# Pair sums behind the transposes, and rotated rows read back from DRAM

## The chip, the cores and the metric

The kernel runs on one core of a Trainium2 chip. The metric is device microseconds of one execution of the whole program (lower is better). The core has five engines that run side by side: TensorE (PE in the profile, with PEld for its weight loads), VectorE (DVE), ScalarE (ACT), GpSimd (POOL) and SyncE (SP, which here only issues transfers). All values are float32.

## The reference, cut to what matters

Eight images of 256 channels and 96 x 96 pixels go through two attention layers, each behind a group norm and with a residual.

```python
# layer 0
x = x + _L0_conv_ref(_gn(x), w1, b1, w2, b2, w3, b3, w_out, temperature)
# layer 1
x = x + _L1_conv_ref(_gn(x), Wq, bq, Wk, bk, Wv, bv)

def _L0_conv_ref(x, ...):
    q_f, k_f, v_f = (fft2(pconv(x, w, b)) for w, b in ((w1, b1), (w2, b2), (w3, b3)))
    # 8 heads of 32 channels; q_f, k_f normalized over the 9216 frequencies
    attn = einsum('bhcn,bhdn->bhcd', q_f, k_f) * temperature
    attn = complex(softmax(real(attn)), softmax(imag(attn)))
    out = abs(ifft2(einsum('bhcd,bhdn->bhcn', attn, v_f)))
    return pconv(out, w_out)

def _L1_conv_ref(x, ...):
    q, k = softplus(Wq x + bq), softplus(Wk x + bk)          # 32 channels
    v = Wv x + bv
    attn_map = einsum('bdn,ben->bde', k, v)
    norm = 1 / einsum('bnd,bd->bn', q, k.sum(-1) + EPS)
    return einsum('bnd,bde,bn->ben', q, attn_map, norm)
```

The product of q_f and k_f has no conjugate, so in pixels it pairs each pixel with its mirror image (row h with row 96 - h, column w with column 96 - w). The kernel therefore needs two Gram matrices of 256 x 256 per image: of e = x + mirrored x, and of o = x - mirrored x, over half of the pixels.

## The kernel before, in words

Channels lie on the 128 partitions, in two halves (KC = 2). Two SBUF arenas hold whole images and swap roles from image to image: one is x, the other holds y of layer 0, later layer 1's k and q, and then takes the next image's x while it is emptied. The rows of an image lie in the arena so that a tile of eight rows t (of NT = 12) holds four rows and their four mirrored rows; `x_col` gives their place. t = 11 is loaded first and t = 0 last.

Each image goes through five stages, and the next image's pair sums are woven into the later ones:

1. **Pair sums** (`pair_sums`): `even_odd` forms e and o for four row pairs at once, with two additions or subtractions of 128 x 760 numbers on POOL or DVE (L317), and small ones for column 0 (L318). Then, 128 pixels at a time, four TensorE transposes (eoT, L350) put the pixels on partitions, ScalarE copies them from PSUM to an xT slot (L353), and eight matmul instructions add their products to the two Gram matrices (acc, L331) one step later. There are 37 such steps per image. Each step also takes its share of the group norm's statistics (L264, DVE).
2. **Attention** (`attention`): a chain of small matmuls and small DVE and ACT operations makes the attention matrix from the Gram matrices, up to `at` (L488) and `mz` (L511).
3. **Rotation** (`rotate`), woven into attention: 48 row pairs. For each, four transposes (xr, L550) put the pixels of the two rows on 96 partitions, ScalarE copies them to an xT slot (L563), and two steps later four y products (L553, two instructions each) multiply them with a window of the table `rt` in DRAM (`tm`, loaded three pairs at a time). DVE copies the result into the y arena (L559) and one column into ys (L558).
4. **Images** (`images`): z (L621) from y, squares and roots, and the projection po (L633) added to x (L635).
5. **Layer 1 and output** (`layer1`, `output`): kq, softplus, kx; then per step four o matmuls (L863), three DVE additions (L868) and one POOL addition (L872) into x, and stores.

The order on the engines comes from generators: `weave(stage, other)` runs as many steps of `other` as the stage yields, so `attention` gives each of its latencies a number of rotation steps, and `images`, `layer1` and `output` do the same with the next image's pair sums; `finish` runs what is left. A planner may reorder instructions outside the blocks of `manual_schedule`; inside them the named engines keep the order of the program: PE in attention, PE, DVE, POOL and SP in the output stage.

```python
        with tc.manual_schedule(engines={mybir.EngineType.PE}):
            weave(attention(b), turns)
            finish(turns)
        sums = pair_sums(b + 1) if b + 1 < B else iter(())
        weave(images(b), sums)
        weave(layer1(b), sums)
```

PSUM has five buffers `ps` for all passing results and three `acc`. SBUF buffers that matter here: the ring of four (e and o tiles, image tiles, weights), three `tm`, and six xT slots, of which the last two serve the pair sums. y's column 0 is copied from x by POOL (L530). x loads, stores, and weights are issued on SP's queue; `tm` for images 1 to 7 on ACT's.

Of the kernel before, what the change touches and what calls it, by code (L numbers as in the profile page):

```python
# [53 lines left out]
P = 128  # L55
KC = 2
# [3 lines left out]
TR = 6  # L60
NZ = 33
# [7 lines left out]
def two_layer_kernel(ctx: ExitStack, tc: tile.TileContext, x, w1t, b1, w2t, b2, w3, b3, wot, temp,  # L69
# [96 lines left out]
    turn = [0, 0]  # L166

    def xt_slot(sums=False):

        turn[sums] += 1  # L170
        return xT[:, NX - 2 + turn[1] % 2 if sums else turn[0] % (NX - 2)]
# [8 lines left out]
    half = const.tile([P, 1], F32, name="half")  # L180
    nc.vector.memset(half, 1.0)
    nc.vector.memset(half[0:W], 0.5 ** 0.5)
# [46 lines left out]
    rt = dram.tile([H, 2 * W], F32, name="rt")  # L229

    def tables():
# [18 lines left out]
        for i in range(2):  # L250
            o = (3 + i) * W
            nc.vector.tensor_copy(t0[:, o:o + 1], r0[:, 0:1])
            nc.vector.tensor_copy(t0[:, o + 1:o + W], r0[:, W - 1:0:-1])
        nc.sync.dma_start(out=rt, in_=t0[:, 3 * W:5 * W])
        load_small()

    def window(h):

        v = rt[h:h + TR, 1:1 + W]
        return bass.AP(v.tensor, v.offset, [[1, W], [2 * W, TR], [1, W]])  # L260

# [34 lines left out]
    def even_odd(b, u):  # L296

        assert (b, u % NT) in loaded
        nr = PR if u < NT else 1
        t = ring_tile(f"eo_{b}_{u}").rearrange("p (c k n) -> p c k n", c=2, k=KC)  # L300
        x_t = image(x_of(b))
        rows = [PR * u + i for i in range(nr)]
        if u in (0, NT):
            parts = [(0, 1)] + ([(1, nr)] if nr > 1 else [])
        else:
            parts = [(0, nr)]
        for lo, hi in parts:
            n = hi - lo
            ra = x_col(rows[lo]) // W
            rp = x_col((H - rows[lo]) % H) // W  # L310
            back = slice(rp, rp - n if rp >= n else None, -1)
            for c in range(2):
                eng = nc.vector if u in (0, 1, NT) or (u == NT // 2 - 1 if b else u % 2) else nc.gpsimd
                op = (eng.tensor_add, eng.tensor_sub)[c]
                pop = (nc.gpsimd.tensor_add, nc.gpsimd.tensor_sub)[c]
                d = t[:, c, :, 0:nr * W].rearrange("p k (h w) -> p k h w", w=W)
                op(d[:, :, lo:hi, 1:W], x_t[:, :, ra:ra + n, 1:W], x_t[:, :, back, W - 1:0:-1])  # L317
                pop(d[:, :, lo:hi, 0:1], x_t[:, :, ra:ra + n, 0:1], x_t[:, :, back, 0:1])  # L318
        return t, nr * W

    s0 = {}

    def pair_sums(b):
# [12 lines left out]

        pending, first = None, True
        us = [*range(NT - 1, -1, -1), NT]
        ahead = [even_odd(b, us.pop(0))]
        for u in range(NT - 1, -2, -1):  # L340
            u %= NT + 1
            eo, cols = ahead.pop(0)
            for i in range(0, cols, P):
                while i == 0 and us and len(ahead) < (2 if b and u in (NT - 3, NT - 4) else 1):
                    ahead.append(even_odd(b, us.pop(0)))
                np_ = min(P, cols - i)
                pt = ps_tile(f"eoT_{b}_{u}_{i}")
                for c in range(2):
                    for k in range(KC):
                        nc.tensor.transpose(pt[0:np_, c * C + k * P:c * C + (k + 1) * P], eo[:, c, k, i:i + np_], ident)  # L350
                t = xt_slot(True)
                weight = half[0:np_] if u in (0, NT) and i == 0 else 1.0
                nc.scalar.activation(t[0:np_, :, 0:C], pt[0:np_, :].rearrange("p (c n) -> p c n", c=2), AF.Copy,  # L353
                                     scale=weight)
                if pending is not None:
                    products(*pending, first, False)
                    first = False
# [608 lines left out]
```

## Time and profile before

| What | Value |
|---|---|
| median of 3 runs | 2763.6 us (2762.03 to 2764.65) |
| the profiled execution's own time | 2762.53 us |
| its span, first to last instruction | 2760.7 us |
| granted TensorE clock, mean | 0.993 |
| PE, PEld, DVE, ACT, POOL busy | 99%, 71%, 71%, 49%, 30% |
| chain that ended last, by engine | PE 94%, DVE 3%, ACT 2%, DMA 1% |
| chain, by line: xr L550, y L553, eoT L350, acc L331 | 6%, 10%, 5%, 13% |
| xr: instructions, mean length | 1520, 275 ns |
| y: instructions, mean length | 3040, 261 ns |
| e and o on POOL, 128 x 760 (L317) | 136, 1809 ns |
| POOL addition of 128 x 384 (L872) | 96, 1004 ns |
| DMA: queues q1 and q10 | 164.34 MB in 129800 packets, 25.12 MB in 67248 |

The profile is of one execution. The busy share of an engine is the time in which it had at least one instruction running. TensorE instructions overlap in the trace, so that the sum or mean of their lengths is more than the time they cost in a row; the spacing of their starts is the better price. The chain follows the last instruction back to what released it at each step. A DMA share is the mean over 16 transfer engines.

### The profile page before, as it was taken

How to read it: one execution, taken by the hardware profiler on the slowest of the kernel's cores; microseconds unless marked ns; L12 is line 12 of the kernel's file. 1: busy time of each engine (PE TensorE's matmuls, PEld its weight loads, DVE VectorE, ACT ScalarE, POOL GpSimd, SP SyncE). 2: the span in 40 equal slices, each digit the busy share in tenths (PEclk: the TensorE clock that was granted, in tenths of full speed). 3: DMA queues.
4: the chain of work that ended last, by engine and by line, in shares of the span. 5: the costliest groups of instructions: out<-in, count | busy, mean ns of one | idle time of the engine just before them, and what ended most of it. 6: DMA issues, size and time to landing. Idle time of an engine off the chain costs nothing.

```text
span 2760.7 us, 47785 instructions
## 1 busy us (share of the span) xinstructions
PE 2719.5 (99%) x18348; PEld 1972.5 (71%) x18348; DVE 1958.4 (71%) x4104; ACT 1366.5 (49%) x2098; POOL 841.5 (30%) x939
## 2 busy tenths in 40 slices
PE   8999999999999999999999999999999999999988
PEld 8965679657795677956679566885678856788556
DVE  7588666876668767587675875769766687676776
ACT  3455634556345563355634546345453455544553
POOL 5033340342403423035230351313513135131311
PEclk9999999999999999999999999999999999999997
DMA  5120151201512015120151201521015210251003
GB/s 169 40 65 11 47 184 43 67 9 49 179 43 73 6 47 182 43 69 6 54 179 46 63 6 54 182 54 52 7 53 184 58 46 7 62 178 28 0 7 138
DMA packets 197274, 192.50 MB, mean 70 GB/s; under 512 B 88821, under 2 KB 197049, under 8 KB 197049
## 3 DMA queue, kind: packets, MB, share of 16 engines
q1 hardware_dynamic: 129800, 164.34, 18.8%
q10 hardware_dynamic: 67248, 25.12, 3.6%
q8 instruction: 146, 2.39, 0.4%
q14 instruction: 80, 0.65, 0.1%
HBM read 113.85 MB, written 75.57 MB: 69 GB/s over the span
## 4 chain that ended last, share of the span: by engine, by line
PE 94%; DVE 3%; ACT 2%; DMA 1%; issue 1%; POOL 0%; SPq 0%; POOLq 0%; DVEq 0%; ACTq 0%
PE z L621 21%; PE po L633 18%; PE acc L331 13%; PE y L553 10%; PE xr L550 6%; PE eoT L350 5%; PE xT L779 5%; PE kq L718 5%; PE o L863 4%; PE kx L755 3%; DMA arena<-in_x_dram 1%; PE cw L423 1%; PE kT L770 1%; DVE arena L559 1%; PE mz L511 1%
## 5 line engine op out<-in xcount | busy, mean ns | idle before, releaser
L621 PE MATMUL z<-arena,mz 128*128 128x384 f32 (+2 forms) x2400 | 595.0, 476 | 0.0
L633 PE MATMUL po<-e,wo 128*128 128x384 f32 x1536 | 529.7, 486 | 0.2 <-ACT e L668 0.2
L667 POOL TENSOR_TENSOR e<-e 128x768 f32<-128x768 f32 x192 | 348.2, 1815 | 554.1 <-ACT e L666 554.1
L621 PEld LDWEIGHTS z<-arena,mz 128*128 128x128 f32 (+1 forms) x2400 | 325.6, 163 | 241.4 <-issue 42.4
L553 PE MATMUL y<-tm,xT 96*128 96x97 f32 x3040 | 472.6, 261 | 1.7 <-ACT sd_a L288 0.5
L553 PEld LDWEIGHTS y<-tm,xT 96*128 96x128 f32 x3040 | 457.8, 192 | 12.5 <-issue 4.9
L331 PE MATMUL acc<-xT 128*128 128x256 f32 (+2 forms) x2368 | 440.5, 328 | 3.5 <-ACT xT L353 3.5
L633 PEld LDWEIGHTS po<-e,wo 128*128 128x128 f32 x1536 | 289.4, 190 | 197.7 <-DVE arena L635 1.2
L662 DVE TENSOR_TENSOR e<-z,xT 128x768 f32<-128x768 f32 x384 | 365.7, 953 | 85.2 <-PE z L621 85.2
L264 DVE BATCH_NORM_STATS2 st<-arena 128x6 f32<-128x384 f32 x768 | 406.5, 552 | 13.7 <-DMA arena<-in_x_dram 3.2
L550 PE MATMUL xr<-ident,arena 128*96 128x128 f32 x1520 | 409.2, 275 | 0.0
L331 PEld LDWEIGHTS acc<-xT 128*128 128x128 f32 (+1 forms) x2368 | 380.2, 191 | 37.7 <-ACT xT L353 5.2
L563 ACT COPY xT<-xr 96x512 f32<-96x512 f32 (+1 forms) x384 | 220.2, 578 | 293.8 <-PE xr L550 289.4
L666 ACT ACTIVATE e<-e 128x1536 f32<-128x1536 f32 x192 | 284.6, 1482 | 93.5 <-DVE e L662 92.3
L668 ACT ACTIVATE e<-e 128x768 f32<-128x768 f32 x192 | 161.9, 843 | 334.0 <-POOL e L667 332.9
L317 POOL TENSOR_TENSOR eo<-arena 128x760 f32<-128x760 f32 x136 | 246.1, 1809 | 253.7 <-issue 130.1
L635 DVE TENSOR_TENSOR arena<-arena,po 128x384 f32<-128x384 f32 x384 | 211.1, 551 | 92.6 <-PE po L633 69.5
L353 ACT ACTIVATE xT<-eoT 128x512 f32<-128x512 f32 x280 | 166.6, 598 | 183.9 <-PE eoT L350 182.2
L550 PEld LDWEIGHTS xr<-ident,arena 128*96 128x96 f32 x1520 | 227.2, 150 | 10.3 <-issue 6.9
L559 DVE COPY arena<-y 128x384 f32<-128x384 f32 (+1 forms) x384 | 209.7, 547 | 1.2 <-issue 0.5
L558 DVE COPY ys<-y 128x4 f32<-128x4 f32 (+1 forms) x384 | 62.4, 162 | 199.3 <-PE y L553 195.9
L350 PE MATMUL eoT<-ident,eo 128*128 128x128 f32 (+1 forms) x1184 | 188.1, 280 | 10.4 <-POOL eo L318 10.4
(202 smaller groups left out, 2907.0 us busy)
## 6 DMA issues: line engine op xcount, KB each, us to landing
arena<-in_x_dram SPq DMA_DIRECT2D x184, 384.0 KB
out_dram<-arena SPq DMA_DIRECT2D x184, 384.0 KB
tm<-rt ACTq DMA_DIRECT2D x112, 216.0 KB
tm<-rt SPq DMA_DIRECT2D x16, 216.0 KB
arena<-in_x_dram SPq DMA_DIRECT2D x8, 288.0 KB
out_dram<-arena SPq DMA_DIRECT2D x8, 288.0 KB
wl<-in_w1t_dram SPq DMA_DIRECT2D x8, 256.0 KB
wl<-in_w2t_dram SPq DMA_DIRECT2D x8, 256.0 KB
```

The source lines that it names most:

```text
L264: nc.vector.bn_stats(out=st[:, k, c, :], in_=x_of(b)[:, k, c * CH:(c + 1) * CH])
L317: op(d[:, :, lo:hi, 1:W], x_t[:, :, ra:ra + n, 1:W], x_t[:, :, back, W - 1:0:-1])
L331: mm = nc.tensor.matmul(acc[c][:, m * C:m * C + (KC - m) * P], lhsT=t[0:np_, c, m * P:(m + 1) * P], rhs=t[0:np_, c, m * P:C], start=(first ...
L350: nc.tensor.transpose(pt[0:np_, c * C + k * P:c * C + (k + 1) * P], eo[:, c, k, i:i + np_], ident)
L550: nc.tensor.transpose(pt[0:W, r * C + k * P:r * C + (k + 1) * P], x_of(b)[:, k, o:o + W], ident)
L553: nc.tensor.matmul(pu[:, o:o + W + 1], lhsT=gt[0:W, r, k * P:(k + 1) * P], rhs=tm[:, g % TR + r, :], start=True, stop=True)
L559: nc.vector.tensor_copy(y[:, :, :, g + r:g + 2], src[:, :, W - 1::-1, r:2])
L621: mm = nc.tensor.matmul(out[:, o:o + n * W], lhsT=columns(mz, k, c, j), rhs=y[:, k, h * W:(h + n) * W], start=(k == 0 and o == 0), stop=(k ...
L633: nc.tensor.matmul(po[:, 0:CH], lhsT=wo[:, k, m * P:(m + 1) * P], rhs=e[:, k, :], start=(k == 0), stop=(k == KC - 1))
L662: nc.vector.tensor_add(e[:, 2 * c:2 * c + 2, :].rearrange("p t (q h) -> p t q h", h=H), pz[:, 0:CH].rearrange("p (q h) -> p q h", h=H).uns ...
L666: nc.scalar.activation(e, e, AF.Square)
L667: nc.gpsimd.tensor_add(e[:, 0:2, :], e[:, 0:2, :], e[:, 2:4, :])
```

## The change

Pair sums: instead of forming e and o and transposing both, each step now transposes 128 pixels of x as they lie in the arena and 128 mirrored pixels, which POOL has copied in reverse order into a small tile `back` (`turn_back`, one step ahead). ScalarE copies both from PSUM into a ring tile, scaled by a column of weights `pw`; e and o are then formed behind it, as sum and difference of the two halves (128 x 256 each), on DVE or on POOL: on POOL for odd j in image 0, and for t < 3 (but for the last step) in the other images. Column 0 of the rows is gathered in a tile `w0` and goes through two mixed chunks at the end, (0, 2) and (0, 3), which POOL puts together from short copies.

For tiles t = 3 to 11 the two halves in the ring tile are stored to a DRAM tile `xtd` (two transfers per step on SP's queue; column 0 by two more behind two transposes of w0). The rotation reads 35 of its 48 row pairs from there into the xT slots (`fetch`, three steps ahead, one transfer of 96 x 2 x 256 numbers, on SP's queue) and does not transpose them; the mirrored rows come in reverse order and are multiplied with a second table `rb`. The row pairs that are still transposed (84 to 94 and 0 to 10, and 48) come first, but for 48. All six xT slots serve the rotation. The two extra tiles of layer 1 (`kxt`) are now taken at the start of the image stage.

```diff
+T0 = 3
...
-    turn = [0, 0]
-    def xt_slot(sums=False):
-        turn[sums] += 1
-        return xT[:, NX - 2 + turn[1] % 2 if sums else turn[0] % (NX - 2)]
+    turn = [0]
+    def sum_slot():
+        turn[0] += 1
+        return xT[:, NX - 2 + turn[0] % 2]
...
+    pw = const.tile([P, 4], F32, name="pw")
+    nc.vector.memset(pw[:, 3:4], 0.0)
...
+    rb = dram.tile([H, 2 * W], F32, name="rb")
+    xtd = dram.tile([2, (H // 2 - PR * T0) * W, C], F32, name="xtd")
...
+            nc.sync.dma_start(out=rb[:, i * W:(i + 1) * W], in_=r0)
...
-    def window(h):
-        v = rt[h:h + TR, 1:1 + W]
-        return bass.AP(v.tensor, v.offset, [[1, W], [2 * W, TR], [1, W]])
+    def window(h, n, back):
+        v = (rb if back else rt)[h:h + n, 0 if back else 1:]
+        return bass.AP(v.tensor, v.offset, [[1, W], [2 * W, n], [1, W]])
+    def turned(c, h, w):
+        return xtd[c, (h - PR * T0) * W + w:]
...
-    def even_odd(b, u):
...
-                op(d[:, :, lo:hi, 1:W], x_t[:, :, ra:ra + n, 1:W], x_t[:, :, back, W - 1:0:-1])
-                pop(d[:, :, lo:hi, 0:1], x_t[:, :, ra:ra + n, 0:1], x_t[:, :, back, 0:1])
...
+        x = x_of(b)
+        w0 = one.tile([P, KC, H + 1], F32, tag="ys", name=f"w0_{b}")
+        nc.gpsimd.memset(w0[:, :, H // 2:H // 2 + 1 + PR * T0], 0.0)
+        def sides(t, j):
+            o = (NT - 1 - t) * TW + (t == 0) * W + 1 + P * j
+            e = (NT - t) * TW - (t == 0) * W - 1 - P * j
+            if t or j < 2:
+                return [(0, P, x[:, :, o:o + P], x[:, :, e:e - P:-1])]
+            m = H // 2
+            rows = [x[:, :, x_col(h):x_col(h) + W] for h in (0, H // 2)] + [w0]
+            if j == 2:
+                return [(0, 32, x[:, :, o:o + 32], x[:, :, e:e - 32:-1])] + [
+                    (32 * i + 32, 32, v[:, :, 1:33], v[:, :, W - 1:W - 33:-1] if i < 2 else w0[:, :, m + 2:m + 34])
+                    for i, v in enumerate(rows)]
+            return [(32 * i, 32, v[:, :, m:m + 32], v[:, :, m:m - 32:-1]) for i, v in enumerate(rows[0:2])] + [
+                (64, 32, w0[:, :, 32:64], None), (64, 16, None, w0[:, :, m + 33:m + 49]), (80, 16, None, w0[:, :, m:m + 16]),
+                (96, 32, rows[0][:, :, 0:32], rows[0][:, :, 0:32])]
+        back = three.tile([P, TR * (W + 1)], F32, tag="tm", name=f"back_{b}")[:, 0:2 * C].rearrange(
+            "p (i k n) -> p i k n", i=2, k=KC)
+        def turn_back(i):
+            t, j = steps[i]
+            assert (b, t) in loaded
+            if j == 0:
+                col = x[:, :, (NT - 1 - t) * TW:(NT - t) * TW:W]
+                h, o = PR * t, H // 2 + 1 + PR * t
+                nc.gpsimd.tensor_copy(w0[:, :, h:h + PR], col[:, :, 0:PR])
+                if t:
+                    nc.gpsimd.tensor_copy(w0[:, :, o:o + PR], col[:, :, :PR - 1:-1])
+                else:
+                    nc.gpsimd.tensor_copy(w0[:, :, o:o + 1], col[:, :, 0:1])
+                    nc.gpsimd.tensor_copy(w0[:, :, o + 1:o + PR], col[:, :, 2 * PR - 2:PR - 1:-1])
+                    nc.gpsimd.tensor_copy(w0[:, :, o - 1:o], col[:, :, 2 * PR - 1:])
+            if j in (0, 3):
+                xts.append(ring_tile(f"xt_{b}_{t}_{j}").rearrange("p (j c n) -> p j c n", j=3, c=2))
+            ab = sides(t, j)
+            ready = len(ab) == 1
+            front = ab[0][2] if ready else xts[-1][:, j % 3, 0].rearrange("p (k n) -> p k n", k=KC)
+            for p0, n, *v in ab:
+                for c in range(ready, 2):
+                    if v[c] is not None:
+                        nc.gpsimd.tensor_copy((front, back[:, i % 2])[c][:, :, p0:p0 + n], v[c])
+            return front, xts[-1][:, j % 3]
+        steps = [(t, j) for t in range(NT - 1, -1, -1) for j in range(3)] + [(0, 3)]
         pending, first = None, True
...
+        xts = []
+        ahead = turn_back(0)
+        for i, (t, j) in enumerate(steps):
+            front, both = ahead
+            if i + 1 < len(steps):
+                ahead = turn_back(i + 1)
+            pt = ps_tile(f"eoT_{b}_{t}_{j}").rearrange("p (c n) -> p c n", c=2)
+            for k in range(KC):
+                nc.tensor.transpose(pt[:, 0, k * P:(k + 1) * P], front[:, k], ident)
+                nc.tensor.transpose(pt[:, 1, k * P:(k + 1) * P], back[:, i % 2, k], ident)
+            nc.scalar.activation(both, pt, AF.Copy, scale=pw[:, j:j + 1])
+            if t >= T0:
+                n = P - j // 2
                 for c in range(2):
-                    for k in range(KC):
-                        nc.tensor.transpose(pt[0:np_, c * C + k * P:c * C + (k + 1) * P], eo[:, c, k, i:i + np_], ident)
-                t = xt_slot(True)
-                nc.scalar.activation(t[0:np_, :, 0:C], pt[0:np_, :].rearrange("p (c n) -> p c n", c=2), AF.Copy,
-                if pending is not None:
-                    products(*pending, first, False)
-                    first = False
-                pending = (t, np_)
-                if u < NT and i:
-                    stats_chunk(st0, b, 2 * (NT - 1 - u) + i // P - 1)
-                yield
+                    nc.sync.dma_start(out=turned(c, PR * t, 1 + P * j)[0:n], in_=both[0:n, c])
+            eo = sum_slot()[:, :, 0:C]
+            if j % 2 if not b else t < T0 and (t or j < 3):
+                nc.gpsimd.tensor_add(eo[:, 0], both[:, 0], both[:, 1])
+                nc.gpsimd.tensor_sub(eo[:, 1], both[:, 0], both[:, 1])
+            else:
+                for c, op in enumerate((ALU.add, ALU.subtract)):
+                    nc.vector.scalar_tensor_tensor(eo[:, c], in0=pt[:, 0], scalar=pw[:, j:j + 1], in1=both[:, 1],
+                                                   op0=ALU.mult, op1=op)
+            if pending is not None:
+                products(*pending, first, False)
+                first = False
+            pending = (eo, P)
+            if j in (1, 2):
+                stats_chunk(st0, b, 2 * (NT - 1 - t) + j - 1)
+            if (t, j) == (T0, 2):
+                n = H // 2 - PR * T0
+                pt = ps_tile(f"w0T_{b}")
+                col = xts[-2][:, 0, 0]
+                for k in range(KC):
+                    nc.tensor.transpose(pt[0:H + 1 - PR * T0, k * P:(k + 1) * P], w0[:, k, PR * T0:H + 1], ident)
+                nc.scalar.copy(col[0:H + 1 - PR * T0], pt[0:H + 1 - PR * T0, 0:C])
+                for c in range(2):
+                    o = c * (H // 2 + 1)
+                    nc.sync.dma_start(out=xtd[c].rearrange("(h w) n -> h w n", w=W)[:, 0], in_=col[o:o + n])
+            yield
...
+            back = H // 2 <= h < H - PR * T0
+            n = 2 if h == H // 2 else 0
+            for lo, hi in ((0, n), (n, TR)) if n else ((0, TR),):
+                (nc.scalar if b else nc.sync).dma_start(out=tm[:, lo:hi, 0:W], in_=window(h + lo, hi - lo, back and lo == n))
             nc.gpsimd.tensor_copy(tm[:, :, W:W + 1], csn[0:W, 2, h:h + TR].unsqueeze(2))
             return tm
 
-        def step(h, turned):
+        order = [*range(H - 2 * TR, H, 2), *range(0, H - 2 * TR, 2)]
+        spilled = [PR * T0 <= h < H - PR * T0 and h != H // 2 for h in order]
+        xts = {}
+        def fetch(i):
+            if i < len(order) and spilled[i]:
+                xts[i] = xT[:, i % NX]
+                h = order[i]
+                c = h > H // 2
+                rows = turned(c, H - h - 1 if c else h, 0)[0:2 * W]
+                nc.sync.dma_start(out=xts[i][0:W, :, 0:C], in_=rows.rearrange("(r w) n -> w r n", w=W))
...
+                back = PR * T0 <= g < H - PR * T0 and g > H // 2
...
-                nc.vector.tensor_copy(y[:, :, :, g + r:g + 2], src[:, :, W - 1::-1, r:2])
+                nc.vector.tensor_copy(y[:, :, :, g + r:g + 2], src[:, :, 0:W, r:2] if back else src[:, :, W - 1::-1, r:2])
...
-        tms = [load_r(g) for g in range(0, 3 * TR, TR)]
+        pieces = order[::TR // 2]
+        tms = [load_r(g) for g in pieces[0:3]]
+        pieces = pieces[3:]
         pending = []
-        for h in range(0, H, 2):
-            if h % TR == 0:
+        for i, h in enumerate(order):
+            if i % (TR // 2) == 0:
                 tm = tms.pop(0)
-            if h % TR == 4 and 3 * TR <= h - 4 + 2 * TR < H:
-                tms.append(load_r(h - 4 + 2 * TR))
-            xt = step(h, pending.pop(0) if len(pending) == 2 else None)
-            pending.append((h, xt, tm))
+            if h % TR == 4 and i > TR // 2 and pieces:
+                tms.append(load_r(pieces.pop(0)))
+            if not spilled[i]:
+                xts[i] = xT[:, i % NX]
+            step(None if spilled[i] else h, pending.pop(0) if len(pending) == 2 else None, xts[i])
+            pending.append((h, xts.pop(i), tm))
+            fetch(i + 3)
...
+        kxt[b] = [three.tile([P, TR * (W + 1)], F32, tag="tm", name=f"xt{i}_{b}")[:, 0:2 * (C + 2)].rearrange(
+            "p (j n) -> p j n", j=2) for i in range(2)]
+        for t in kxt[b]:
+            nc.gpsimd.memset(t[:, :, C:C + 2], 1.0)
...
-        extra = [three.tile([P, TR * (W + 1)], F32, tag="tm", name=f"xt{i}_{b}")[:, 0:2 * (C + 2)].rearrange(
-            "p (j n) -> p j n", j=2) for i in range(2)]
-        for t in extra:
-            nc.gpsimd.memset(t[:, :, C:C + 2], 1.0)
...
```

## The prediction

> **What bounds the kernel now.** I read the busy shares first, then the chain of waits, then TensorE's waits, then the timeline where the change acts.
>
> ```profile
> PE 2719.5 (99%) x18348; PEld 1972.5 (71%) x18348; DVE 1958.4 (71%) x4104; ACT 1366.5 (49%) x2098; POOL 841.5 (30%) x939
> PE 94%; DVE 3%; ACT 2%; DMA 1%; issue 1%; POOL 0%; SPq 0%; POOLq 0%; DVEq 0%; ACTq 0%
> PE eoT L350 <- POOL eo L318: 10.4, 15, 7.3
> PE at L488 <- DVE arena L559: 1.1, 7, 0.2
> ```
>
> TensorE is busy 99% and is 94% of the chain that ended last. The two waits (total us, times, longest) say that it hardly ever waits, but the second shows a place where seven images arrive with no slack: the attention matmul `at` is just late for VectorE. So work taken off TensorE is worth its issue time, wherever nothing else becomes late.
>
> How much issue time is a transpose? The busy column misleads: the rows of L550 (409.2 us) and L553 (472.6) count overlapping instructions. I take start-to-start times (start, length, engine, instruction), at the end of one image's rotation:
>
> ```profile
> 486.05 0.27 PE L550 MATMUL xr<-ident,arena 128*96 128x128 f32 x1
> 486.17 0.36 PE L553 MATMUL y<-tm,xT 96*128 96x97 f32 x2
> 486.36 0.27 PE L550 MATMUL xr<-ident,arena 128*96 128x128 f32 x1
> 486.47 0.36 PE L553 MATMUL y<-tm,xT 96*128 96x97 f32 x2
> 486.67 0.27 PE L550 MATMUL xr<-ident,arena 128*96 128x128 f32 x1
> 486.78 2.15 PE L553 MATMUL y<-tm,xT 96*128 96x97 f32 x18
> ```
> ```profile
> 486.67 2.09 PEld L553 LDWEIGHTS y<-tm,xT 96*128 96x128 f32 x18
> ```
>
> One transpose plus one y product (two instructions) takes 0.31 us; a row pair has four of each, 1.24 us. In the last line 18 y instructions run without transposes: (2.15 - 0.26)/17 = 0.111 us each, and the weight loads keep the same pace, (2.09 - 0.19)/17 = 0.112. So y alone is bound by its weight loads, and a pair without transposes costs 8 x 0.111 = 0.89 us. Taking four transposes away saves **0.35 us per pair**, not the 0.45 that four times their 0.11 spacing suggests.
>
> **What the Trainium skill says.** "Perfetto Trace Analysis", Identifying the Most-Contended Engine: matmul busy share is a poor measure, weight-load share a better one; here 99% against 71%, and the overlap above agrees. "TensorE: Matmul & The Clock Gate", LDWEIGHTS: columns/1.2 ns, so 107 ns for 128 columns; the 112 ns above agrees. "GPSIMD Engine Reference", 3.1 Elementwise: 2.6 cycles per element for two inputs, 2.2 ns at its 1.2 GHz; the trace's (1815 - 1004)/384 = 2.1 ns per element (768- and 384-wide adds, L667 and L872) agrees. [...]
>
> **Part 1, rotation: the gain.** In the built program the xr transposes fall from 1520 to 400: 35 pairs x 4 x 8 images = 1120. 35 x 0.35 x 8 = **-98 us**. The 280 ScalarE copies of 0.58 us that go too were hidden behind TensorE.
>
> **Part 2, what the rotation uncovers: +32.** Attention's latencies are hidden behind rotation steps, and 36 of the 48 become shorter. Between `ssq` and `at` VectorE works without a break in the timeline: 10.5 us for reciprocals, softmax pieces and seven or eight y copies (0.54 us per pair back to back), in nearly the same order in the new program. TensorE covers it today with eight 1.24 us steps; at 0.89 it arrives 2.8 us early, of which I keep 2 as a wait. The short hops after it (one step of cover each) give 1 more. The fetches: each brings 192 packets of 1 KB. Queue q1 spent 18.8% of 16 engines' span on 129800 packets, 64 ns for 1266 B; at 1 KB I estimate 52 to 64 ns, so 0.62 to 0.77 us of all 16 engines per pair. The `tm` windows (q10: 23.6 ns x 576 packets per three pairs) add 0.28. Sum 0.90 to 1.05 against 0.89 on TensorE: in the last 16 pairs, where no attention work is left, the transfers are level with TensorE or a little slower[...]. I take 1. Together 4 us per image (bounds 1.5 and 8).
>
> **Part 3, pair sums in mid-image: +14 for seven images.** Transposes (4 per step, 37 steps) and acc products are the same. What moves is before and behind them. POOL gets one reversed 128x256 copy per step: 0.34 us by the slope of its small copies, 0.65 by L530's strided 128x192 copy (0.525 us); I take 0.4. e and o, formerly one set of large operations per three steps, come behind ScalarE's copy: two VectorE operations of 128x256, estimated 0.36 us each from the 0.49 spacing of the 384-wide adds of L868. In the output stage (the 40 us before attention):
>
> ```profile
> 712.00:720.00 8.00, 8.00 (x60) 5.68 (x59) 5.44 (x13) 2.96 (x7) 4.33 (x6) 1.00 0.61 203
> 720.00:728.00 8.00, 8.00 (x61) 5.71 (x60) 6.05 (x14) 2.97 (x7) 6.52 (x6) 1.00 1.03 374
> 728.00:736.00 8.00, 8.00 (x61) 5.71 (x60) 7.32 (x14) 2.98 (x6) 6.53 (x9) 1.00 0.87 313
> 736.00:744.00 8.00, 8.00 (x57) 6.29 (x56) 6.37 (x14) 3.19 (x7) 3.33 (x4) 1.00 0.80 268
> 744.00:752.00 8.00, 8.00 (x57) 7.53 (x56) 7.47 (x16) 2.88 (x5) 2.91 (x7) 1.00 0.94 324
> ```
>
> Columns: window, length, PE, PEld, DVE, ACT, POOL busy, clock, DMA share, GB/s. A step takes TensorE 2.67 us here. VectorE has three adds (1.47), statistics (1.0 in two steps of three, 0.67 on average) and now 0.72: 2.86. So it is late by 0.2 per step for eight steps, and by about as much where softplus fills it in layer 1. 2 us per image (0.5 to 3.5).
>
> **Part 4, the end of the sums: +52 for seven images, the term that decides.** For t < 3 the adds are POOL's, and this stretch has no slack. Per step in the output stage POOL has 1.0 (L872), 0.4 (copy) and two adds of 193 + 256 x 2.1 = 730 ns: 2.9, with the column copies 3.3, against TensorE's 2.67; lag 1 us after four steps. Then six steps follow alone, 1.75 us each on TensorE (the spacing of eoT starts at 743.10, 744.85, 746.60). POOL has in order: six pairs of adds (8.7), three copies (1.2), four column copies (0.8), eight and nine small copies for the two mixed chunks at about 0.2 (3.4), and L530's copy (0.5), which the new program places before the last two pairs of adds: 14.6 us. The last of these adds must be done before its products, which without waits start 10.9 us after the first transposes; POOL starts 1.3 us behind those plus the lag, so it ends at 16.9: 6 us late. L530's copy waits for the output stores:
>
> ```profile
> 742.12 1.00 POOL L872 TENSOR_TENSOR arena<-arena,po 128x384 f32<-128x384 f32 x1 [1.82 <-ACT po L871]
> 744.41 2.53 POOL L318 TENSOR_TENSOR eo<-arena 128x2 f32<-128x2 f32 x6 [1.28 <-DMA arena<-in_x_dram]
> 750.65 0.52 POOL L530 COPY arena<-arena 128x192 f32<-128x192 f32 x1 [3.71 <-DMA out_dram<-arena]
> ```
>
> Today it stands last and delays nobody; these stores end at 750.65 with DMA already at 0.80 to 1.03 of its 16 engines. Twelve spills and two column spills ahead of them on SP's queue (0.43 us each of 16 engines at the price above) push them 3 to 5 us later, so POOL may wait 1 to 3 us at it, the later adds and TensorE's products behind it. The load of x rows t=0 (the second line: POOL waited 1.28 us for it) is behind the same queue. I take 7.5 us per image (4 to 11).
>
> **Part 5, image 0 and small things: +15.** Its sums run alone at 1.75 us per step, so products can start 2.19 us after their transposes. Behind a transpose come ScalarE (start 0.70, 0.60 long), then two POOL adds of 0.73: 2.85, so 12 POOL steps lose 0.7 each; VectorE's steps just fit (2.1). With start and mixed chunks 13 us (5 to 18). The two w0T transposes per image: 2 us in all. SP issues 54 spills and 35 fetches more per image at 0.37 to 0.48 us, about 37 us of an image's 340; it is in order, so stores and loads behind a spill wait for its ScalarE copy, priced in part 4. The column copies in the image stage (0.2 us each, waiting for loads) stand before POOL's e adds, which sit idle 3 us before each one today: nothing.
>
> **Sum** against the profiled execution (2762.5 us; span 2760.7 plus 1.8 around it): -98 + 32 + 14 + 52 + 13 + 2 = +15, so 2777.5. The median of the runs is 1.1 higher: **2778 us**.
>
> **Rivals.**
> - The gain wins. The same mechanisms at their lower sizes: attention 2 us per image, the tail 3, mid-image 1, image 0 10: -98 + 16 + 21 + 7 + 10 + 2 = -42, 2721. It turns where parts 2 to 4 cost less than some 11 us per image together. For it: POOL idles 70% over the span, and its lengths are rough. Against: POOL's serial order at the tail. 30%.
> - The fetches set the pace. If a pair takes DMA 1.24 us, the whole gain of part 1 is lost and attention's waits with it: 2762 + 14 + 52 + 15 = 2844. For it: 0.90 to 1.05 is close. Against: the share is 0.2 in that stage today. 7%.
> - They cancel, within 0.2% (5.5 us, about what a measurement can tell from no change): 10%.
> - That the transposes are not removed is excluded by the counts above.
>
> **Numbers.** My own case, slower by up to some 70 us: 53%. Faster 0.30, same 0.10, slower 0.60. All costs at their low ends give 2716, all at the high ends 2850; the range is 2715 to 2835.
>
> **What would show it.** Right: y instructions 0.11 us apart in runs of eight; `PE eoT` or `PE acc` waiting for POOL 6 us or more at each image's end, and POOL busy throughout there; a wait of about 2 us at `at`. Wrong: no TensorE wait for POOL at the tail (then it is faster by 40), y waiting for `xT<-xtd` transfers (then the second rival), or y pairs of 0.78 us.

## The result, and the profile after

The changed kernel takes **3173.6 us** (median of 4 runs, 3167.7 to 3179.9) against 2764.1 on the same chip: ratio 1.148, 95% interval 1.145 to 1.151. It is slower by 409 us; forecast were 2778 and a range up to 2835. The profiled execution took 3176.3 us, its span 3174.5.

The busy shares, the chain of waits by engine and then by line, and two rows of the DMA issues (count, KB each), from the page of the changed kernel:

```profile
PE 2789.5 (88%) x17244; PEld 2007.0 (63%) x17244; DVE 2056.1 (65%) x4467; ACT 1230.9 (39%) x1826; POOL 809.2 (25%) x1363
PE 73%; DMA 15%; SPq 4%; DVE 2%; ACT 2%; POOL 1%; issue 1%; POOLq 0%; ACTq 0%; DVEq 0%
PE z L712 18%; PE po L724 15%; PE y L635 10%; DMA xtd<-xt 10%; PE acc L328 7%; PE xT L866 4%; PE kq L809 4%; DMA xT<-xtd 3%; PE kx L846 2%; DMA arena<-in_x_dram 2%; SPq L401 2%; SPq L969 2%; PE o L950 2%; PE xr L632 1%; PE eoT L395 1%
xtd<-xt SPq DMA_DIRECT2D x288, 128.0 KB
xtd<-xt SPq DMA_DIRECT2D x144, 127.0 KB
```

TensorE's share of the chain fell from 94% to 73%. DMA rose from 1% to 15%, and 10% is one line, `DMA xtd<-xt`, the spill of the turned rows. A third of the spills have 127 rows, not 128: with j = 2 the change writes `n = P - j // 2` rows. Who waits is in TensorE's waits (total us, times, longest), with one wait of ScalarE from the waits of all engines:

```profile
PE eoT L395 <- ACT xt L422: 120.8, 7, 17.3
PE eoT L395 <- DMA arena<-in_x_dram: 85.2, 8, 12.3
PE acc L328 <- DVE xT L408: 77.7, 20, 21.1
PE at L553 <- DVE scr L550: 27.6, 9, 3.7
PE eoT L396 <- POOL back L382: 13.1, 16, 2.1
PE y L635 <- DMA xT<-xtd: 12.7, 22, 1.2
PE acc L328 <- POOL xT L404: 11.0, 10, 9.2
ACT xt L422 <- DMA xtd<-xt: 156.8, 8, 23.1
```

In the first line seven images wait 17 us each for L422, the ScalarE copy of the column that is spilled last. The last line says what that copy waits for: spills. It writes into a ring tile whose spills must have landed. The wait for x rows (second line) is new, as TensorE has no such wait in the kernel before: the loads stand behind the spills on SP's queue. What DMA does in such a pause is in windows of image 0 (window, length, busy time of PE, PEld, DVE, ACT, POOL, granted clock, DMA share, GB/s):

```profile
64.00:66.00 2.00, 0.00 (x0) 0.00 (x0) 0.00 (x0) 0.09 (x1) 0.00 (x0) 1.00 0.07 24
68.00:70.00 2.00, 2.00 (x9) 1.73 (x8) 0.51 (x2) 0.00 (x0) 0.00 (x0) 0.50 0.07 24
76.00:78.00 2.00, 0.00 (x0) 0.00 (x0) 0.00 (x0) 0.00 (x0) 0.00 (x0) 0.50 0.07 24
```

A DMA share of 0.07 is the busy time of about one of 16 engines: while everything waits for transfers, as good as fifteen of sixteen transfer engines are idle. At 24 GB/s 127 KB take 5.4 us, where the prediction priced a spill at 0.43. The clock column shows a second effect: in the second window, behind a pause, TensorE works at 0.50 of its clock.

### The profile page after: what moved, and what is told of

Read it like the earlier page. It is cut to its first block, busy times and chain, and to the rows that moved or that the text cites. A ratio compares the mean times of both kernels' runs of the same rounds, so it can differ in the third digit from the quotient of the medians.

```text
span 3174.5 us, 47627 instructions
## 1 busy us (share of the span) xinstructions
PE 2789.5 (88%) x17244; PEld 2007.0 (63%) x17244; DVE 2056.1 (65%) x4467; ACT 1230.9 (39%) x1826; POOL 809.2 (25%) x1363
## 4 chain that ended last, share of the span: by engine, by line
PE 73%; DMA 15%; SPq 4%; DVE 2%; ACT 2%; POOL 1%; issue 1%; POOLq 0%; ACTq 0%; DVEq 0%
PE z L712 18%; PE po L724 15%; PE y L635 10%; DMA xtd<-xt 10%; PE acc L328 7%; PE xT L866 4%; PE kq L809 4%; DMA xT<-xtd 3%; PE kx L846 2%; DMA arena<-in_x_dram 2%; SPq L401 2%; SPq L969 2%; PE o L950 2%; PE xr L632 1%; PE eoT L395 1%
## 5 line engine op out<-in xcount | busy, mean ns | idle before, releaser
L328 PE MATMUL acc<-xT 128*128 128x256 f32 (+1 forms) x2368 | 479.3, 348 | 89.9 <-DVE xT L408 77.7
L328 PEld LDWEIGHTS acc<-xT 128*128 128x128 f32 x2368 | 405.4, 203 | 143.4 <-DVE xT L408 85.9
L635 PE MATMUL y<-tm,xT 96*128 96x97 f32 x3040 | 446.4, 298 | 19.0 <-DMA xT<-xtd 12.7
L635 PEld LDWEIGHTS y<-tm,xT 96*128 96x128 f32 x3040 | 432.6, 217 | 31.9 <-POOL xt L700 8.4
L397 ACT ACTIVATE xt<-eoT,pw 128x512 f32<-128x512 f32 x296 | 201.7, 687 | 397.3 <-PE eoT L396 288.3
L395 PE MATMUL eoT<-ident,arena 128*128 128x128 f32 x560 | 153.7, 299 | 206.0 <-ACT xt L422 120.8
L408 DVE SCALAR_TENSOR_TENSOR xT<-eoT,pw,xt 128x256 f32<-128x256 f32 x440 | 191.3, 475 | 201.0 <-ACT xt L397 195.3
L395 PEld LDWEIGHTS eoT<-ident,arena 128*128 128x128 f32 x560 | 83.3, 149 | 278.1 <-issue 138.8
L955 DVE TENSOR_TENSOR arena<-arena,o 128x384 f32<-128x384 f32 x288 | 141.7, 547 | 155.4 <-PE o L950 155.3
L382 POOL COPY back<-arena 128x256 f32<-128x256 f32 (+1 forms) x328 | 129.6, 397 | 387.6 <-PE eoT L396 387.4
```

The source lines that it names most:

```text
L328: mm = nc.tensor.matmul(acc[c][:, m * C:m * C + (KC - m) * P], lhsT=t[0:np_, c, m * P:(m + 1) * P], rhs=t[0:np_, c, m * P:C], start=(first ...
L395: nc.tensor.transpose(pt[:, 0, k * P:(k + 1) * P], front[:, k], ident)
L397: nc.scalar.activation(both, pt, AF.Copy, scale=pw[:, j:j + 1])
L635: nc.tensor.matmul(pu[:, o:o + W + 1], lhsT=gt[0:W, 1 - r if back else r, k * P:(k + 1) * P], rhs=tm[:, g % TR + r, :], start=True, stop=True)
```

## Experiments

Fourteen kernels, each timed against the kernel before on its own chip unless said. "Per image" is the time from the first to the last instruction of a stage in TensorE's timeline: before, 135 us of sums (from the first to the last L350, with all that lies between), 72 us of rotation (first to last y), 125 us of the z stage. The edits are cut: `...` stands for lines left out, among them those that give every spill 128 rows in the kernels from section 2 on.

### 1. The 127-row spills

Three kernels: 127 rows made 128 by a padded buffer (row 128 is overwritten later or never read); transfers of different row counts alone, with no other work; and the j = 1 spill cut into 127 rows and 1.

```diff
-    xtd = dram.tile([2, (H // 2 - PR * T0) * W, C], F32, name="xtd")
+    xtd = dram.tile([2, (H // 2 - PR * T0 + 1) * W, C], F32, name="xtd")
...
-                n = P - j // 2
+                n = P
...
```

> Every spill has 128 rows: the third chunk of a tile also stores its last row (a row of zeros that falls on a column-0 row, which the w0T transfer writes later); xtd has room for it. Bytes grow by less than 1%. Theory A (the changed kernel loses its time to the 144 spills of 127 rows, each of which runs on one of the 16 transfer engines: DMA share 0.07 and 24 GB/s while everything waits): those waits go, and what is left is the prediction's sum, about 2778 us, anywhere from 2700 to 2830. Theory B (the 112 MB of added traffic collides with loads and stores): within 1% of the changed kernel's 3174 us. Theory C (POOL and VectorE behind the transposes are too slow for the pair sums): also near 3174 us.

> No part of the computation: only transfers of n rows of 1 KB between SBUF and DRAM, four in a row for each n, each waiting for the one before. It leaves out the whole reference. Theory A: 128 rows take about 2 to 2.5 us each from start to start, 127 rows 5.4 us (127 KB at 24 GB/s) plus about 2, and other counts are fast or slow by how many engines their factors allow: 126 (2 x 63) and 124 (4 x 31) between, 112 (16 x 7) as fast as 128; 127 rows split into 112 + 15 near 2 to 3 us. Theory B and C: all between 1.8 and 2.5 us, by bytes; 127 like 128.

```diff
                 n = P - j // 2
                 for c in range(2):
+                    if j == 1:
+                        n = P - 1
+                        nc.sync.dma_start(out=turned(c, PR * t, P * j + P)[0:1], in_=both[n:P, c])
...
```

> The changed kernel with the middle chunk of each tile stored as 127 rows and one row, so that there are 288 spills of 127 rows instead of 144; bytes are the same. Theory A: 144 more transfers of 5.4 us on one engine are 97 us per image; the first 144 cost some 410 us in all, so another 400 to 780: 3570 to 3950 us. Theories B and C: the 144 small transfers more cost SP 0.4 us each, under 60 us in all: 3170 to 3230 us.

With 128 rows: 2921.7 us, ratio 1.0555 (1.0534 to 1.0575), 252 us under the change. With twice as many 127-row spills, a single run: 3826.9 us, so 653 us more for 144 of them, 4.5 us each, in which the 144 transfers of one row are contained. Taking the 127-row spills away and doubling them go the same way; doubled, most of their 5.4 us shows, as made part of it lay beside other work (252 us for 144). The second of the three kernels measures a transfer directly. Each size was moved four times, one after another; the groups of SP's issues by tile (length of an issue in ns, then first and last start) and then windows over four 127-row writes and over four of 127 rows of 4 KB (window, length, busy time of DVE and POOL, granted clock, DMA share, GB/s):

```profile
L81 SPq DMA_DIRECT2D w128rows<-src x4: 320/327/348, 2.0 to 7.1; - x4
L81 SPq DMA_DIRECT2D w127rows<-src x4: 216/222/334, 7.5 to 29.1; - x4
L81 SPq DMA_DIRECT2D w125rows<-src x4: 249/250/306, 40.7 to 49.2; - x4
L81 SPq DMA_DIRECT2D w120rows<-src x4: 316/316/356, 59.6 to 66.1; - x4
L81 SPq DMA_DIRECT2D w96rows<-src x4: 304/306/359, 78.6 to 83.8; - x4
7.50:29.30 21.80, 0.00 (x0) 0.00 (x0) 1.00 0.07 24
153.80:230.50 76.70, 0.00 (x0) 0.00 (x0) 1.00 0.06 24
```

From first to last start are three intervals: 1.7 us each for 128 rows, **7.2 for 127**, 2.8 for 125, 2.2 for 120, 1.7 for 96. For 126 rows, one fewer, it is 1.8 from the second transfer on (the first stood behind the last write of 127). Rows four times as long do not help: still 24 GB/s. The same 127 rows written as 112 and 15, two transfers, took 1.9 us for both. So the row count decides, not the bytes. The Trainium skill states the rule: "DMA: Bandwidth & Descriptors", Why a DMA increments its semaphore by 16 and not by 1: a transfer runs on the largest number of engines up to 16 that divides the slowest dimension of both its sides, and 127 partitions give 1. The 0.07 above agrees, and so does 126 = 9 x 14, for which the expectation had wrongly named a time in between.

But 128 rows left 157 us over the kernel before, more than was expected. The next runs split that.

### 2. Sums alone, spills, fetches

```diff
# e5: nothing is read back; e4: nothing is written either
-        spilled = [PR * T0 <= h < H - PR * T0 and h != H // 2 for h in order]
+        spilled = [False for h in order]
...
-            back = H // 2 <= h < H - PR * T0
-            n = 2 if h == H // 2 else 0
+            back, n = False, 0
...
# e4, besides
-            if t >= T0:
+            if False:
...
-            if (t, j) == (T0, 2):
+            if False:
```

> The new pair sums alone: nothing is written to DRAM or fetched, and every row pair is transposed in the rotation as before the change (rows of 128 kept). What is computed is the same. Theory T (what is left of the loss after the 127-row spills are mended lies in transfers: spills and output stores share the transfer engines, the last x tiles land late, and TensorE's pauses cost a stretch at half clock afterwards): without any transfer the sums take about as long as before, 134 to 137 us an image, and the time is 2750 to 2800. Rival E (the engine work itself: the second VectorE operation per step and the GpSimd chain of copy, add and subtract in the last three tiles bound the sums, +14 and +52 of the prediction): the sums stay at 143 to 148 us an image and the time is 2815 to 2870.

> Spills of 128 rows and the column store stay, but nothing reads them: the rotation transposes every row pair from x as before the change. Against the version without transfers the difference is what the spills cost; against the version with spills of 128 rows and fetches (2921.7) it is what the fetched rotation gains. Theory T: the spills cost 8 to 13 us an image in the output stage, so 2830 to 2890 in all, and the fetched rotation, 77 us where the transposing one took 72, is a loss of 30 to 60 us. Rival E: spills cost under 20 us in all against the version without transfers, and the rest of the 157 us is in the sums without them. Rival G (the fetched rotation does gain, and the spills hide it): above 2950.

Sums alone: 2817.7 us, ratio 1.0192 (1.0175 to 1.0209); with spills of 128 rows that nobody reads: 2870.3, ratio 1.0378 (1.0362 to 1.0393). In steps of the ratio, at 2764.6 us:

| step | added |
|---|---|
| the new sums, no transfers | +53 us |
| spills of 128 rows | +51 us |
| the rotation fetches 35 pairs | +49 us |
| a third of the spills with 127 rows | +256 us |

Each step is measured with the steps above it in place. Both theories were half right: the sums' own work costs 53 us (rival E), and transfers of 128 rows cost as much twice over (theory T). TensorE's waits of the two kernels show the spills' part, sums alone first:

```profile
PE acc L328 <- DVE xT L408: 15.5, 14, 1.6
PE acc L328 <- POOL xT L404: 5.5, 16, 0.5
PE eoT L395 <- DMA arena<-in_x_dram: 4.9, 1, 4.9
```
```profile
PE eoT L395 <- DMA arena<-in_x_dram: 29.0, 8, 4.9
PE acc L328 <- DVE xT L408: 26.6, 17, 9.8
```

With spills every image from the second on waits 3.4 us for its last x rows (the wait of 4.9 us is image 0's, with and without spills). Their load stands behind stores and spills while DMA runs at 1.0 and 340 to 350 GB/s, and TensorE then works some microseconds at half clock: 147 us of sums for 141. In image 0 one wait for a ring tile of spills lasted 12.5 us (ScalarE's L397), and the sums ended 13 us later. Here the transfer engines were not full: TensorE stood still from 58.2 us on, and up to 62 us their share was 0.08 to 0.11. SP's timeline shows what the spills stood behind: from 41.1 to 62.2 us it issued 53 small loads of biases and weights, one after another, and no spill (start, length, issue):

```profile
35.69 3.84 SPq L401 DMA_DIRECT2D xtd<-xt  x8
51.36 10.80 SPq L230 DMA_DIRECT2D wo<-in_wot_dram  x32
62.27 9.74 SPq L401 DMA_DIRECT2D xtd<-xt  x20
```

So some 13 of the 51 us are a matter of SP's order of issue, as the timeline has it; no run changed that order.

Why the sums alone lose: the rotation behind them begins 6.8 us later per image in the mean of images 1 to 7, and 5.5 later in image 0, which makes the 53 us. Counted from the end of the z stage, TensorE's eoT steps are 2.5 us late where the output stage begins (93.1 us for 90.6), 3.2 when the last six steps begin, 6.2 in the mean at the last. The timeline shows at the first place VectorE's reciprocal (L911, 2.56 us) with the e and o operations behind it, at the last GpSimd's small copies for the two mixed chunks (eight at 0.18 us, then nine, each set followed by adds of 0.74). That these are the causes is read from the timeline and not tested; the runs of section 4 speak against two others.

### 3. Why the fetched rotation does not gain

The rotation with fetches took 77 us an image, with three of four transposes gone. TensorE's timeline in one rotation of the 128-row version:

```profile
1215.10 0.78 PE L553 MATMUL at<-gsel,scr 128*128 128x132 f32 x2 [4.27 <-DVE scr L550]
1215.67 5.28 PE L635 MATMUL y<-tm,xT 96*128 96x97 f32 x24
1239.44 2.89 PE L635 MATMUL y<-tm,xT 96*128 96x97 f32 x24 [0.44 <-POOL tm L604]
1242.77 3.13 PE L635 MATMUL y<-tm,xT 96*128 96x97 f32 x24 [0.44 <-POOL tm L604]
1246.52 2.02 PE L635 MATMUL y<-tm,xT 96*128 96x97 f32 x16 [0.61 <-DMA xT<-xtd]
1249.18 7.11 PE L635 MATMUL y<-tm,xT 96*128 96x97 f32 x32 [0.64 <-DMA xT<-xtd]
```

Three things. `at` waits 4.3 us. The 24 y behind it take 0.22 us each, twice their price: half clock, which lasts until 1228.7. And from 1239 to 1249 eight pairs need 9.74 us, 1.22 each, with small waits for windows and fetches, at a DMA share of 1.14; then half clock again (32 in 7.11 us).

> Spills of 128 rows with fetches, and seven more rotation steps in TensorE's order ahead of the first at matmul (yield 12 where it was 5). Theory T: the pause of 4.3 us at the at matmul and the 12 us at half clock that followed it (24 matmuls in 5.3 us where full clock takes 2.7) go: 8 to 10 us an image, so 2840 to 2860. Rival F (fetches and window loads bound the rotation anyway, the pause only moved): within 15 us of 2921.

```diff
-            yield (5, 3)[m]
+            yield (12, 3)[m]
```

2864.1 us, ratio 1.0367 (1.0333 to 1.0401): 52 us less in steps of the ratio, 4 us above the range expected; the rotation takes 68 to 74 us, and `at` still waits up to 2.0 us. With fewer fetches and no spill near the output stage:

```diff
-T0 = 3
+T0 = 6
...
-            if j % 2 if not b else t < T0 and (t or j < 3):
+            if j % 2 if not b else t < 3 and (t or j < 3):
```

> Spills of 128 rows for the first six tiles of the sums instead of nine (T0 = 6; the GpSimd adds stay in the last three): 23 of 48 pairs fetched, and no spill lies in the output stage, where output stores already keep the transfer engines at 0.9 to 1.1. Theory T: the sums come back to 135 to 139 us an image, the rotation has a longer cover for the at chain and takes 66 to 72 us: 2700 to 2790. Rival E: sums stay at 145 to 148, 2830 to 2900.

> T0 = 6 (23 pairs fetched, no spill in the output stage) and seven more rotation steps ahead of the first at matmul. Theory T (a pause of TensorE costs its length and then a stretch at half clock): the rotation, 74 us an image in the version with T0 = 6 alone, loses the 2.8 us pause and the slow matmuls behind it and takes 62 to 66 us: 25 pairs at 1.5 us and 23 at 0.9 to 1.0 us, so 2745 to 2780. Rival F (fetches and window loads set the rotation's pace): it stays within 20 us of 2840.

> T0 = 5 in place of 6 with the later at matmul and without the spreading: 27 pairs fetched, one more tile spilled. Theory T: 4 more pairs at 0.5 us less each, 16 us in all, less 0 to 16 us as the spill comes nearer the output stage: 2735 to 2785, within 16 us of the version with T0 = 6. Rival S (any more spills reach the stage where stores fill the transfer engines): over 16 us slower than it.

T0 = 6 alone: 2840.0 us (1.0252 to 1.0282); the sums come back to 141 us, those without transfers, so the spills are hidden there; but the rotation took 74, and 2790 was missed. With the later `at`: 2787.8 (ratio 1.0053 to 1.0095), 8 us above the range expected. The rotation is 66 to 71 us in seven images and 76 in one. T0 = 5: 2819.8, 32 us slower than T0 = 6 (here row pair 76 takes the turned table in place of the straight one; the work is the same). That is rival S's size but not its place: the sums stay at 141 us, so the added spills are hidden too. The rotation is longer, 72 us in the mean for 69: TensorE waits for `at` 13.7 us in all, up to 2.0 at a time, where with T0 = 6 it is 5.2 and up to 0.9.

The two lengths of one program's rotation led to a last question: are the fetches, in one block, what makes TensorE pause? The same work was put in another order, pieces of three pairs from DRAM and pieces transposed alternating; `at` comes two more steps later (`yield (14, 3)`).

```diff
-        order = [*range(H - 2 * TR, H, 2), *range(0, H - 2 * TR, 2)]
+        order = [*range(H - 2 * TR, H, TR), *range(0, H - 2 * TR, TR)]
+        far = [h for h in order if PR * T0 <= h < H - PR * T0]
+        near = [h for h in order if h not in far]
+        order, k = [], len(far) / (len(near) - 1)
+        for i, h in enumerate(near):
+            order += [h] + far[round(i * k):round((i + 1) * k)]
+        order = [h + r for h in order for r in range(0, TR, 2)]
```

> The version of 2787.8 (T0 = 6, later at matmul) with the rotation's order of six-row pieces changed: pieces read from DRAM and pieces transposed alternate, where they stood in two blocks (the at matmul two steps later again). The work is the same. Theory T (in the block of fetched pairs the transfers, at 1.1 and 240 GB/s, don't keep up with y alone; TensorE then idles a fifth of the time and is put to half clock for 20 us in most images, 76 us of rotation where an undisturbed image took 66): with the fetches spread the pace is kept, no half-clock stretch, rotation 60 to 64 us: 2720 to 2760, under the time before. Rival F2 (the fetched pairs are slow for another reason, or the half-clock stretch comes from the at wait): 2775 to 2800.

> The change's own T0 = 3 (35 of 48 pairs fetched, spills of 128 rows), later at matmul, pieces interleaved. Theory T: the rotation, 68 to 73 us in blocks, takes 56 to 63 us, the sums keep the 6 us an image that spills in the output stage cost: 2760 to 2815 against 2864 in blocks. Rival F2: 2850 to 2870.

At the change's own T0 = 3 it is 2801.2 us, ratio 1.0136 (1.0107 to 1.0166), 63 us under 2864: the rotation takes 61 us in four images, 65 or 66 in four, and TensorE no longer waits for `at`, and 0.7 us in all for fetches (13.7 and 11.1 us with blocks). No run parts the order's share of this from that of the two steps for `at`. At T0 = 6 it is 2793.1 (1.009 to 1.0127), no better than in blocks: a miss for theory T, and in the range that rival F2 named. The expectation had put the loss in blocks at 20 us of half clock in most images; the trace had 24 us in one image and 3 to 10 in four. In the new order `at` no longer waits; a transposed pair stands in its place, whose ScalarE copy waits behind the softmax. The first matmuls behind that pause in images 1 and 6 (start, length; the wait in brackets), and a window of 4 us in each some microseconds later:

```profile
455.71 2.03 PE L641 MATMUL y<-tm,xT 96*128 96x97 f32 x16 [1.05 <-ACT xT L650]
2175.51 3.05 PE L641 MATMUL y<-tm,xT 96*128 96x97 f32 x16 [1.05 <-ACT xT L650]
```
```profile
457.00:461.00 4.00, 4.00 (x39) 4.00 (x39) 3.75 (x16) 0.58 (x1) 0.38 (x2) 1.00 0.44 110
2180.00:2184.00 4.00, 4.00 (x21) 4.00 (x21) 1.25 (x4) 0.58 (x1) 0.19 (x1) 0.50 0.05 4
```

The pause is 1.05 us in both. Image 1 goes on at full clock, 39 instructions in 4 us, and its rotation takes 66 us; image 6 gets half clock, 21 in 4 us, and takes 73. Of the five images with this pause three kept the clock (66 us) and two lost it (71 and 73); image 0 had no pause (65), images 2 and 3 had pauses of 1.33 and 2.08 us and lost it too (73). So a small pause costs its length, or some 6 us more.

### 4. The sums' work spread otherwise

In images 1 to 7 GpSimd subtracts o in mid-image, and ScalarE makes the turned copy in the last three tiles.

```diff
+                        if ready and b and t < 3:
+                            nc.scalar.copy(back[:, i % 2], v[c])
...
+                if b:
+                    nc.gpsimd.tensor_sub(eo[:, 1], both[:, 0], both[:, 1])
...
```

> The same spreading with no transfer at all (the version of 2817.7, rotation transposing every pair). Theory E': 2765 to 2790. Rival: above 2805.

> The version before, and in images 1 to 7 the work on the sums spread otherwise: o is subtracted by GpSimd in the middle of the image (VectorE makes only e), and in the last three tiles the turned copy is made by ScalarE (GpSimd keeps add and subtract). Theory E' (the 52 us that the sums alone lost come from VectorE's second operation and from the GpSimd chain of copy, add, subtract and the output add L959 that fills its 2.85 us): 30 to 50 us below the version before, 2700 to 2745. Rival (they come from work on TensorE's own line, so no spreading helps): within 12 us of it.

> The version before with o subtracted by GpSimd in the middle of images 1 to 7 and the turned copy by ScalarE in their last three tiles. The spreading was worth 7 us without transfers: 2712 to 2755, 4 to 12 us under the version before.

Without transfers 2810.7 us (ratio 1.0146 to 1.0183), 7 below; on the two T0 = 6 versions 9 and 6 us below, at 2778.5 and 2787.4. In all three the intervals overlap with those of the version before. The rival's number holds, so spreading the second VectorE operation and the turned copy in this way gives back some 7 of the 53 us and no more. The rival's reason, work on TensorE's own line, is not shown by it. The best version, 2778.5 us (ratio 1.0033 to 1.0068), is still slower than the kernel before; none beat it.

## Why the prediction was wrong

The direction was right, the size was not: +15 us forecast, +409 measured. By its steps:

- **The step that failed** stands in part 4: twelve spills and two column spills "0.43 us each of 16 engines". Four of those twelve have 127 rows and run on one engine for 5.4 us. The other 42 spills of an image, 14 of them with 127 rows, got no price beyond SP's time to issue them. The price was an average over q1's packets in a kernel whose large transfers the prediction took to use all 16 engines, carried over to a transfer of another shape. The row count was in the diff, and the rule in the section of the skill named above. The 144 spills of 127 rows alone are 256 of the 409 us.
- **Spills with 128 rows** were priced only as a delay of L530's copy, 1 to 3 us an image within part 4. They cost 51 us: the load of the last x rows behind them, the ring tiles that they hold in image 0, and slow matmuls after. The prediction named the load and gave it no price; it had loads and stores wait behind spills on SP's queue, but not spills behind loads, as in image 0.
- **Part 1**, -98 us: the mechanism and nearly the size hold. Undisturbed rotations take 61 us where 72 were (interleaved, T0 = 3): 11 us an image, against 12.2.
- **Part 2**, +32 us, is the other wrong term. The rotation takes 3 us more than before in the change as made (76 for 72 in the mean) and 5 us more with spills of 128 rows, instead of 8 less. The wait at `at` was 3.4 us, not 2; a fetched pair with its window took 1.22 us, not 0.90 to 1.05, so windows and fetches set the pace in the last block; and pauses were followed by half clock (13 us of slow matmuls behind the one at `at` shown above), which the prediction has nowhere. It counted a wait as its length.
- **Part 3**, +14 us: 2.5 us an image were lost ahead of the output stage, 18 in all. The operation took 0.475 us, not 0.36.
- **Part 4 without transfers**, +52 us: 4.3 us an image more until the rotation begins, 30 in all. POOL's prices were right (copy 0.397 us, add 0.727), its lag was not: the waits for POOL are short.
- **Part 5**, +13 for image 0: its rotation began 5.5 us later. With the two before, that makes the 53 us.

Parts 3 to 5 together were 81 us forecast and 53 measured; the rotation -66 and +49; the spills, priced only inside part 4, cost 307. The rival "the fetches set the pace" named 1.24 us a pair, close to the 1.22 measured in the last block, and got 7%. Of the signs named beforehand, the long waits for POOL at each image's end did not come (11.0 and 13.1 us for the whole kernel, in the lines of its waits above), yet the kernel was not "faster by 40", as that sign was to mean: the time lay in a term without a sign. `y` waits for `xT<-xtd`, but only 1.6 us an image; its larger cost is in the clock. That the direction was right is in part luck: most of the 409 us is a cost that the sum does not hold. The high ends of its own costs gave 2850 and this rival 2844, and the range stopped at 2835.

## What to carry to other kernels

Before pricing a transfer, factor its row count: one row less than 128 turned 1.7 us into 7.2, and padding by a row gave back 252 us. When a new transfer joins an in-order queue (here SP's) or holds a shared buffer (here the ring), follow all who stand behind it, and what it stands behind. On a TensorE that is busy 99% a pause may cost several times its length, so work taken off it gains only if everything else keeps its pace. Alternating the short pieces with long ones, with `at` two steps later, was worth 63 us at T0 = 3 and nothing at T0 = 6.

## What the runs showed of the hardware

- A write of 127 rows moves at 22 to 24 GB/s, at the busy time of about one engine, with rows of 1, 2 and 4 KB; a read of 127 rows of 1 KB at 23 GB/s.
- Half clock after short pauses. The Trainium skill ("TensorE: Matmul & The Clock Gate", Part 1: The HAM clock gate) says half rate after an idle window of about 3.4 us, free-running, and full rate after a busy one. The traces agree with the window: in each of them the granted clock changes only on one grid of 3.413 us, from the first change to the last (564 changes in the 15 traces of whole kernels, none more than 0.006 us off its grid). They do not agree with "idle" and "a busy one", and there the measurement decides. These are windows on that grid in the interleaved kernel with T0 = 6, two of image 1 and then four of image 6, and one from T0 = 6 in blocks (columns as above):

```profile
452.56:455.97 3.41, 2.36 (x22) 2.19 (x21) 3.11 (x13) 2.61 (x5) 0.19 (x1) 1.00 0.58 166
455.97:459.39 3.42, 3.42 (x34) 3.42 (x33) 3.02 (x16) 0.94 (x3) 0.19 (x1) 1.00 0.57 156
2172.88:2176.29 3.41, 2.36 (x22) 2.19 (x21) 3.03 (x15) 2.17 (x4) 0.00 (x0) 1.00 0.62 178
2176.29:2179.70 3.41, 3.41 (x19) 3.41 (x18) 3.04 (x15) 0.42 (x2) 0.19 (x1) 0.50 0.49 130
2186.53:2189.94 3.41, 3.41 (x19) 3.41 (x18) 1.25 (x4) 0.97 (x2) 0.19 (x1) 0.50 0.18 58
2189.94:2193.36 3.42, 3.42 (x33) 3.42 (x33) 2.04 (x7) 0.58 (x1) 0.19 (x1) 1.00 0.46 122
```
```profile
1162.90:1166.32 3.42, 3.42 (x14) 3.01 (x13) 1.12 (x3) 0.00 (x0) 0.19 (x1) 0.50 0.45 121
```

Each pause of 1.05 us lies whole in one window, in which TensorE is busy 2.36 of 3.41 us in both images; image 6 loses the clock in the next window and image 1 keeps it. So where the pause falls on the grid does not explain the difference; what does stays open. Half clock then lasts four windows, 14 us, with TensorE busy throughout; in the last line it is the seventh such window, 24 us in all (the rotation of 76 us). In all 15 traces, the first 12 us left out, a window with TensorE busy under 0.4 was followed by half clock 137 times of 137, one with 0.82 or more 2 times of 11,141, and in between both happened (90 times of 491).
